# A row scan of nine-tap convolutions, with its columns kept in three phases and six sub-products of three taps in place of nine taps

## Chip, core and metric

The kernel is one program on one core of a Trainium2 chip. TensorE multiplies (PE; its weight loads are listed apart as PEld), VectorE (DVE), ScalarE (ACT) and GpSimd (POOL) work element by element, and SyncE (SP) issues most of the DMA transfers. The metric is the device time of one execution in microseconds (us), as the median of the runs shown. The profile is one other execution, recorded by the hardware profiler.

## What is computed

Four layers in a row on a float32 image batch of 4 x 128 x 128 x 128 (batch, rows, columns, channels), each as `x = x + layer(groupnorm(x))`. The first is a deformable convolution, the third a message layer, the fourth a triangle product. The change is made for the second, a scan over the 128 rows:

```
rows = jnp.moveaxis(x, 1, 0)
def step(carry, row):
    new = row + jax.nn.relu(conv1d_same(carry, W))     # 9 taps along the columns, 128 -> 128 channels
    return (new, new)
_, outs = jax.lax.scan(step, rows[0], rows[1:])
```

Each row needs the finished row before it, so the rows can't be worked side by side; the four batches can.

## The kernel before, in words

`scan_layer` (from line 966) holds channels on the 128 partitions. Per row and batch, 128 columns lie along the free dimension.

- **Loading.** `rows(y0)` (line 994) fetches four rows of layer 1's output at a time: four transfers on SP's queue, one for each batch, each 128 columns (the partitions) by four rows of 512 bytes. It is called one chunk ahead, at the first row of the chunk before.
- **Turning.** `turned` (line 1003) transposes each batch's 128 x 128 block on PE into one PSUM tile `x1T_ps`, and ACT writes the normalized row `rowT` from it, one instruction for each batch (line 1011).
- **Convolving.** The carry of one row is kept in two halves of two batches each, twice (old and new), with four zero columns at either side. For each half, nine matmuls of 256 columns (2 batches x 128) add up in one PSUM bank (line 1029). Float32 matmuls run as two passes, so the profile shows 18 of them for each half, 36 for a row.
- **Closing the row.** DVE writes the new carry half as `max(conv, 0) + rowT` (line 1040) and the layer's output `x2c` as that plus the raw row, read from `x1T_ps` (line 1045). Every fourth row DVE also takes statistics of `x2c` (line 1049), its sums over the columns (`sum_w`, line 1053) and over the rows (`part`, `sum_h`, lines 1055 and 1056), and ACT's queue issues four stores of `x2c` (line 1052).

The order within each engine is set by a scheduler from the tiles' dependences, and semaphores join the engines. While PE works on one half of a row, DVE closes the other half. PSUM has eight banks: four for `x1T_ps`, four for the convolution.

`message_and_triangle` (from line 1061) reads `x2c` back as `X`, batch by batch. Its `right` (line 1240, POOL) and its output transfers (line 1315) are the only other places that the change touches.

Of the kernel before, what the change touches and what calls it, by code (L numbers as in the profile page):

```python
# [9 lines left out]
F32 = mybir.dt.float32  # L10
# [3 lines left out]
ALU = mybir.AluOpType  # L14
AX = mybir.AxisListType
PSUM = bass.MemoryType.PSUM
DRAM = bass.MemoryType.DRAM

P = 128
B = 4  # L20
S = 128
# [9 lines left out]
TAPS = 9  # L31
NQ = 4
DQ = P // NQ
# [929 lines left out]
                nc.vector.tensor_copy(to, v)  # L963


def scan_layer(tc, c, small, x1, w, norms, x2T):

    nc = tc.nc  # L970
    RB = 4
    PAD = TAPS // 2
    WP = S + 2 * PAD
    HB = B // 2
    stats = small.tile([P, B, S // RB, 6], F32, name="stats2")
    sum_w = small.tile([P, B, S], F32, name="sum_w")
    sum_h = small.tile([P, B, S], F32, name="sum_h")
    nc.vector.memset(sum_h, 0.0)
    with ExitStack() as ctx:
        wp = ctx.enter_context(tc.tile_pool(name="l1w", bufs=1))  # L980
        two = ctx.enter_context(tc.tile_pool(name="l1two", bufs=2))
        three = ctx.enter_context(tc.tile_pool(name="l1three", bufs=3))
        ps_x = ctx.enter_context(tc.tile_pool(name="l1ps_x", bufs=4, space=PSUM))
        ps_c = ctx.enter_context(tc.tile_pool(name="l1ps_c", bufs=4, space=PSUM))

        wt = wp.tile([P, TAPS, P], F32, name="wconv")
        nc.scalar.dma_start(wt, w.rearrange("k i o -> i k o"))
        carry = [
            [wp.tile([P, HB, WP], F32, name=f"carry_{i}_{h}") for h in range(2)] for i in range(2)
        ]  # L990
        for pair in carry:
            for t in pair:
                nc.vector.memset(t, 0.0)

        def rows(y0):
            xc = three.tile([P, B, RB, S], F32, name="x1rows")
            for b in range(B):
                nc.sync.dma_start(
                    xc[:, b], x1[b, y0 : y0 + RB, :, :].rearrange("h w c -> w h c")
                )  # L1000
            return xc

        def turned(xc, i):

            px = ps_x.tile([P, B, S], F32, name="x1T_ps")
            for b in range(B):
                nc.tensor.transpose(px[:, b, :], xc[:, b, i, :], c.ident)  # L1007
            rt = three.tile([P, B, S], F32, name="rowT")
            for b in range(B):
                s, t = norms[b]  # L1010
                nc.scalar.activation(rt[:, b, :], px[:, b, :], AF.Identity, bias=t, scale=s)  # L1011
            return px, rt

        chunks = {0: rows(0)}
        ready = {0: turned(chunks[0], 0)}
        for y in range(S):
            i = y % RB
            if i == 0:
                x2c = two.tile([P, B, RB, S], F32, name="x2c")
                if y + RB < S:  # L1020
                    chunks[y + RB] = rows(y + RB)
            px, rt = ready.pop(y)
            old, new = carry[(y + 1) % 2], carry[y % 2]
            conv = []
            if y:
                for h in range(2):
                    pc = ps_c.tile([P, HB, S], F32, name="conv1_ps")
                    for k in range(TAPS):
                        nc.tensor.matmul(  # L1029
                            pc, lhsT=wt[:, k, :], rhs=old[h][:, :, k : k + S],  # L1030
                            start=(k == 0), stop=(k == TAPS - 1),
                        )
                    conv.append(pc)
            if y + 1 < S:
                ready[y + 1] = turned(chunks[(y + 1) // RB * RB], (y + 1) % RB)
            for h in range(2):
                bs = slice(h * HB, (h + 1) * HB)
                mid = new[h][:, :, PAD : PAD + S]
                if y:
                    nc.vector.scalar_tensor_tensor(  # L1040
                        mid, conv[h], 0.0, rt[:, bs, :], ALU.max, ALU.add
                    )
                else:
                    nc.vector.tensor_copy(mid, rt[:, bs, :])
                nc.vector.tensor_tensor(x2c[:, bs, i, :], px[:, bs, :], mid, ALU.add)
            if i == RB - 1:
                y0 = y + 1 - RB
                for b in range(B):
                    nc.vector.bn_stats(
                        stats[:, b, y // RB, :], x2c[:, b].rearrange("p h w -> p (h w)")  # L1050
                    )
                    nc.scalar.dma_start(x2T[b, :, y0 : y + 1, :], x2c[:, b])
                nc.vector.tensor_reduce(sum_w[:, :, y0 : y + 1], x2c, AX.X, ALU.add)
                part = two.tile([P, B, S], F32, name="part")
                nc.vector.tensor_reduce(part, x2c.rearrange("p b h w -> p b w h"), AX.X, ALU.add)
                nc.vector.tensor_tensor(sum_h, sum_h, part, ALU.add)
                chunks.pop(y0)
    return stats, sum_w, sum_h


def message_and_triangle(tc, c, x2T, counted, w2, w3, out):
# [3 lines left out]
    nc = tc.nc  # L1065
    stats2, sum_w, sum_h = counted
# [3 lines left out]
    JB = 8  # L1070
    with ExitStack() as ctx:
        wp = ctx.enter_context(tc.tile_pool(name="l3w", bufs=1))
# [30 lines left out]
        with tc.tile_pool(name="l3prep", bufs=1) as prep, tc.tile_pool(  # L1103
            name="l3ps_w", bufs=2, space=PSUM
        ) as ps_w:
            raw = prep.tile([P, NP_], F32, name="wraw")
# [3 lines left out]
            both = ((left_w, left_b), (right_w, right_b), (lgate_w, lgate_b), (rgate_w, rgate_b))  # L1110
# [30 lines left out]
        one = ctx.enter_context(tc.tile_pool(name="l3one", bufs=1))  # L1141
        two = ctx.enter_context(tc.tile_pool(name="l3two", bufs=2))
        ps_s = ctx.enter_context(tc.tile_pool(name="l3ps_s", bufs=2, space=PSUM))
        ps_a = ctx.enter_context(tc.tile_pool(name="l3ps_a", bufs=4, space=PSUM))
        ps_b = ctx.enter_context(tc.tile_pool(name="l3ps_b", bufs=2, space=PSUM))

        for b in range(B):
# [5 lines left out]
            _, _, s2, t2 = gn_part(nc, c, two, two, ps_s, stats2[:, b], "x2")  # L1153
# [47 lines left out]
            for j0 in range(0, S, 4):  # L1201
                py = ps_a.tile([P, S, 4], F32, name="cent_ps", tag="ps_a")
                nc.tensor.matmul(  # L1203
                    py, lhsT=c.center, rhs=X[:, :, j0 : j0 + 4], start=True, stop=True
# [3 lines left out]
                for j in range(4):  # L1208
                    nc.tensor.matmul(  # L1209
                        pv[:, j0 + j : j0 + j + 1], lhsT=sq[:, j, :], rhs=c.mean[:, 0:1],  # L1210
                        start=True, stop=True,
# [7 lines left out]
            for q in range(NQ):  # L1219
                left = big.tile([P, S, DQ], F32, name=f"left_{q}")  # L1220
                right = big.tile([P, S, DQ], F32, name="right")
                cols = slice(q * 4 * DQ, (q + 1) * 4 * DQ)
                for j0 in range(0, S, 4):
                    pp = ps_a.tile([P, 4, 4 * DQ], F32, name="proj_ps", tag="ps_a")
                    for j in range(4):
                        nc.tensor.matmul(  # L1226
                            pp[:, j], lhsT=X[:, :, j0 + j], rhs=wcat[:, cols], start=True, stop=True
                        )
                    pre = two.tile([P, 4, 4 * DQ], F32, name="work")
                    for j in range(4):  # L1230
                        nc.vector.scalar_tensor_tensor(  # L1231
                            pre[:, j], pp[:, j], rstd[:, j0 + j : j0 + j + 1], pbias[:, cols],
                            ALU.mult, ALU.add,
                        )
                    sig = two.tile([P, 4, 2 * DQ], F32, name="sig")
                    nc.scalar.activation(sig, pre[:, :, 2 * DQ :], AF.Sigmoid)  # L1236
                    nc.vector.tensor_tensor(
                        left[:, j0 : j0 + 4, :], pre[:, :, 0:DQ], sig[:, :, 0:DQ], ALU.mult
                    )
                    nc.gpsimd.tensor_tensor(  # L1240
                        right[:, j0 : j0 + 4, :], pre[:, :, DQ : 2 * DQ], sig[:, :, DQ:], ALU.mult
                    )
                for d0 in range(0, DQ, 4):
                    pt = ps_b.tile([P, 4, S], F32, name="tri_ps", tag="ps_b")
                    for d in range(4):
                        nc.tensor.matmul(  # L1246
                            pt[:, d], lhsT=right[:, :, d0 + d], rhs=left[:, :, d0 + d],
                            start=True, stop=True,
                        )
                    nc.scalar.copy(left[:, :, d0 : d0 + 4], pt.rearrange("p d j -> p j d"))  # L1250
                prod.append(left)
# [3 lines left out]
            for j0 in range(0, S, JB):  # L1255
# [21 lines left out]
                for h in range(0, JB, 4):  # L1277
                    pg = ps_a.tile([P, 4, P], F32, name="gate_ps", tag="ps_a")
                    for j in range(4):
                        nc.tensor.matmul(  # L1280
                            pg[:, j], lhsT=X[:, :, j0 + h + j], rhs=wcat[:, gcols],
                            start=True, stop=True,
# [16 lines left out]
                res = two.tile([P, JB, P], F32, name="res")  # L1299
                for h in range(0, JB, 4):  # L1300
# [11 lines left out]
                    nc.vector.tensor_tensor(  # L1312
                        res[:, h : h + 4], po, lastb.unsqueeze(1).to_broadcast([P, 4, P]), ALU.add
                    )
                nc.sync.dma_start(out[b, :, j0 : j0 + JB, :], res)


@with_exitstack
# [67 lines left out]
```

## Time and profile before

| what | us |
|---|---|
| median of 3 runs (8645.82 to 8707.95) | 8695.24 |
| span of the profiled execution | 8803.9 |
| of it, the scan: first load issued to the last carry written | 4489.8 to 5543.0 |
| PE busy over the span | 7117.6 (81%) |
| DVE busy over the span | 5000.0 (57%) |
| ACT busy over the span | 3346.5 (38%) |
| POOL busy over the span | 1721.0 (20%) |

The profiled execution spans 108.7 us more than the median of the timed runs; what lies around its span isn't shown apart. The profile's slices say how much of each fortieth of the span an engine was busy, and the timeline lists instructions by start and duration with, in brackets, how long the engine had been idle and what released it. A matmul's duration holds the way through the array, so matmuls in a row overlap: their pace is read from start to start.

### The profile page before, as it was taken

How to read it: one execution, taken by the hardware profiler on the slowest of the kernel's cores; microseconds unless marked ns; L12 is line 12 of the kernel's file. 1: busy time of each engine (PE TensorE's matmuls, PEld its weight loads, DVE VectorE, ACT ScalarE, POOL GpSimd, SP SyncE). 2: the span in 40 equal slices, each digit the busy share in tenths (PEclk: the TensorE clock that was granted, in tenths of full speed). 3: DMA queues.
4: the chain of work that ended last, by engine and by line, in shares of the span. 5: the costliest groups of instructions: out<-in, count | busy, mean ns of one | idle time of the engine just before them, and what ended most of it. 6: DMA issues, size and time to landing. Idle time of an engine off the chain costs nothing. (4 is left out here: it accounts for less than half of the span.)

```text
span 8803.9 us, 105220 instructions
## 1 busy us (share of the span) xinstructions
PE 7117.6 (81%) x35800; PEld 5835.4 (66%) x35800; DVE 5000.0 (57%) x13104; ACT 3346.5 (38%) x5404; POOL 1721.0 (20%) x1791
## 2 busy tenths in 40 slices
PE   0668777978789777799989999698679668966986
PEld 0556565756567556677778888398549647963985
DVE  5545555755557555577744444447626752674466
ACT  0445554555555555466621111122312312231223
POOL 0123222233222223222200000112112120212121
PEclk9778887988878888799999999688759876976897
DMA  2333333433333333343321221100100010001000
GB/s 66 88 67 77 76 74 69 98 76 80 73 72 98 72 74 76 68 80 61 64 65 60 67 67 54 53 1 10 42 25 1 20 58 1 1 29 48 1 10 29
DMA packets 978744, 473.48 MB, mean 54 GB/s; under 512 B 705076, under 2 KB 931988, under 8 KB 963860
## 3 DMA queue, kind: packets, MB, share of 16 engines
q1 hardware_dynamic: 951216, 428.93, 20.3%
q10 hardware_dynamic: 26980, 37.73, 1.2%
q8 instruction: 284, 4.65, 0.2%
q14 instruction: 264, 2.16, 0.1%
HBM read 284.15 MB, written 182.35 MB: 53 GB/s over the span
## 5 line engine op out<-in xcount | busy, mean ns | idle before, releaser
L491 PEld LDWEIGHTS v_ps<-m,pixels 120*128 120x128 f32 x11008 | 1512.9, 206 | 221.5 <-issue 69.3
L473 ACT ACTIVATE dist<-t_ps 120x780 f32<-120x780 f32 x1560 | 1266.5, 812 | 983.6 <-DVE neg L481 848.5
L491 PE MATMUL v_ps<-m,pixels 120*128 120x108 f32 (+1 forms) x11008 | 1610.0, 291 | 20.1 <-DVE v L502 14.9
L502 DVE COPY v<-v_ps 128x432 f32<-128x432 f32 x1376 | 809.6, 588 | 1390.4 <-PE v_ps L491 1386.9
L551 PE MATMUL conv_ps<-v,wneg 128*128 128x128 f32 (+2 forms) x5160 | 1382.6, 403 | 14.8 <-DVE v L507 14.8
L482 POOL TENSOR_TENSOR m<-neg,tent 120x390 f32<-120x390 f32 x688 | 700.9, 1019 | 2785.1 <-DVE neg L481 2508.1
L551 PEld LDWEIGHTS conv_ps<-v,wneg 128*128 128x128 f32 x5160 | 851.6, 205 | 305.5 <-issue 181.6
L1029 PE MATMUL conv_ps<-carry,wconv 128*128 128x256 f32 x4572 | 1009.5, 378 | 0.3 <-issue 0.3
L1029 PEld LDWEIGHTS conv_ps<-carry,wconv 128*128 128x128 f32 x4572 | 850.8, 188 | 121.3 <-issue 0.6
L475 ACT ACTIVATE tent<-dist 120x390 f32<-120x390 f32 x1560 | 823.0, 528 | 213.7 <-POOL m L482 155.9
L1226 PE MATMUL proj_ps<-wcat,X 128*128 128x128 f32 x4096 | 903.0, 384 | 0.0
L1226 PEld LDWEIGHTS proj_ps<-wcat,X 128*128 128x128 f32 x4096 | 901.5, 313 | 0.0
L1231 DVE SCALAR_TENSOR_TENSOR work<-proj_ps,rstd,pbias 128x128 f32<-128x128 f32 x2048 | 613.2, 344 | 293.3 <-issue 173.7
L464 PE MATMUL t_ps<-places,spread 14*120 14x390 bf16 x3096 | 581.4, 388 | 214.2 <-ACT dist L473 166.1
L482 DVE TENSOR_TENSOR m<-neg,tent 120x390 f32<-120x390 f32 x860 | 652.1, 758 | 91.1 <-DVE neg L481 1.4
L481 DVE TENSOR_SCALAR neg<-dist 120x390 f32<-120x390 f32 x1560 | 630.9, 414 | 42.2 <-ACT dist L473 41.2
L464 PEld LDWEIGHTS <-spread 14*120 14x120 bf16 x3120 | 221.8, 129 | 515.8 <-issue 414.8
L1011 ACT ACTIVATE rowT<-x1T_ps,t_x,s_x 128x128 f32<-128x128 f32 x512 | 192.4, 458 | 862.7 <-PE x1T_ps L1007 417.2
L371 PE MATMUL img_ps<-ident,xin 128*128 128x128 f32 x512 | 98.1, 325 | 514.4 <-DMA xin<-in_x_dram 511.5
L1240 POOL TENSOR_TENSOR right<-work,sig 128x128 f32<-128x128 f32 x512 | 240.6, 471 | 1362.4 <-ACT sig L1236 1138.0
L1303 PE MATMUL gT_ps<-ident,cen 128*128 128x128 f32 x512 | 124.0, 424 | 468.5 <-DVE cen L1298 412.1
L1236 ACT ACTIVATE sig<-work 128x256 f32<-128x256 f32 x512 | 213.4, 417 | 639.1 <-DVE work L1231 639.1
(185 smaller groups left out, 8134.4 us busy)
## 6 DMA issues: line engine op xcount, KB each, us to landing
pixels<-tab SPq DMA_DIRECT2D x688, 120.0 KB
xin<-in_x_dram SPq DMA_DIRECT2D x56, 1024.0 KB
tab<-rows SPq DMA_DIRECT2D x384, 128.0 KB
x<-x1c SPq DMA_DIRECT2D x32, 1024.0 KB
x1rows<-x SPq DMA_DIRECT2D x128, 256.0 KB
x2T<-x2c ACTq DMA_DIRECT2D x128, 256.0 KB
X<-x2T SPq DMA_DIRECT2D x16, 2048.0 KB
out_dram<-res SPq DMA_DIRECT2D x64, 512.0 KB
```

The costliest lines, as they stand in the source:

```text
L464: nc.tensor.matmul(tp[0:LANES, d, 0:n].rearrange("p (r c) -> p r c", c=PADW), lhsT=spread[p0 : p0 + 14, :], rhs=src[p0 : p0 + 14, k, :, 0: ...
L473: nc.scalar.activation(dist[:, :, 0:n], tp[0:LANES, :, 0:n], AF.Abs)
L475: nc.scalar.activation(tent[:, 0:n], dist[:, 0, 0:n], AF.Relu, bias=1.0, scale=-1.0)
L481: nc.vector.tensor_scalar(neg[:, 0:n], dist[:, 1, 0:n], 1.0, 1.0, ALU.min, ALU.subtract)
L482: engine.tensor_tensor(m, neg[:, 0:n], tent[:, 0:n], ALU.mult)
L491: nc.tensor.matmul(vp[:, h * n : h * n + rows * w].rearrange("p (k c) -> p k c", c=w), lhsT=pix[0:LANES, xb, :], rhs=m[:, :, RX * xb : RX ...
L502: nc.vector.tensor_copy(v[:, :, c0 : c0 + full * RX].rearrange("p k (h c) -> p k h c", c=RX), vp[:, 0 : full * n].rearrange("p (h k c) -> ...
L551: nc.tensor.matmul(pc[:, at : at + r1 - r0, :], lhsT=wneg[:, 3 * ky + kx, :], rhs=v[:, k0 + kx, r0:r1, kx : kx + S], start=m == 0, stop=m ...
L1029: nc.tensor.matmul(pc, lhsT=wt[:, k, :], rhs=old[h][:, :, k : k + S], start=(k == 0), stop=(k == TAPS - 1),)
L1226: nc.tensor.matmul(pp[:, j], lhsT=X[:, :, j0 + j], rhs=wcat[:, cols], start=True, stop=True)
L1231: nc.vector.scalar_tensor_tensor(pre[:, j], pp[:, j], rstd[:, j0 + j : j0 + j + 1], pbias[:, cols], ALU.mult, ALU.add,)
L1240: nc.gpsimd.tensor_tensor(right[:, j0 : j0 + 4, :], pre[:, :, DQ : 2 * DQ], sig[:, :, DQ:], ALU.mult)
```

## The change

The columns are kept by their number modulo three: phase 0 has 43 of them, phase 1 43 and phase 2 42. Written so, a nine-tap convolution is a three-by-three arrangement of three-tap convolutions of phases, and a known identity forms the three output phases from six three-tap products in place of nine, some of them on sums of phases and with sums of weights. Each product takes all four batches at once: 172 columns (176 for the one named `edge`), three matmuls, two passes each.

- The carry becomes one tile for all batches with six slots: the three phases (0, 1, 2) and three sums (3 = 0+1, 4 = 1+2, 5 = 0+1+2).
- DVE closes a row with twelve instructions of 172 elements in place of four of 256, and ACT copies one product (`m1`) out of PSUM first.
- The output `x2c` and the sums over rows move to POOL: three additions of 172 elements and one of 512 a row. ACT makes a copy `raw` of the turned row for it, as POOL is given no PSUM tile.
- `rows` loads each batch in three transfers, one for each phase, of 43, 43 and 42 partitions. Two chunks are loaded before the first row, and each later chunk is called for at the first row of the chunk before it, as until now. The stores of `x2c` go from ACT's queue to SP's.
- An order written by hand (`manual_schedule`) makes each engine run the scan's instructions in the order of the program text.
- Later, `right` and the output are put back into natural column order: `right` in two POOL instructions where a group of columns crosses a phase, and the output in transfers of 512-byte pieces.

```diff
+        less2 = wp.tile([P, PHASES, P], F32, name="less2")
+        nc.vector.tensor_scalar(less2, taps[:, 2], -1.0, None, ALU.mult)
...
             for b in range(B):
-                nc.sync.dma_start(
-                    xc[:, b], x1[b, y0 : y0 + RB, :, :].rearrange("h w c -> w h c")
-                )
+                for p in range(PHASES):
+                    nc.sync.dma_start(
+                        xc[FIRST[p] : FIRST[p] + COUNT[p], b],
+                        x1[b, y0 : y0 + RB, p:S:PHASES, :].rearrange("h w c -> w h c"),
+                    )
...
+            raw = three.tile([P, B, S], F32, name="rawT")
+            nc.scalar.copy(raw, px)
+            return rt, raw
...
+        def product(to, terms):
+            n = to.shape[2]
+            todo = [(wgt[:, a], src, at + a) for wgt, src, at in terms for a in range(PHASES)]
+            for i, (wgt, src, at) in enumerate(todo):
+                nc.tensor.matmul(
+                    to, lhsT=wgt, rhs=src[:, :, at : at + n],
+                    start=i == 0, stop=i + 1 == len(todo),
+                )
...
+        ctx.enter_context(tc.manual_schedule(engines=order))
+        chunks = {0: rows(0), RB: rows(RB)}
...
             if y:
-                for h in range(2):
-                    pc = ps_c.tile([P, HB, S], F32, name="conv1_ps")
-                    for k in range(TAPS):
-                        nc.tensor.matmul(
-                            pc, lhsT=wt[:, k, :], rhs=old[h][:, :, k : k + S],
-                            start=(k == 0), stop=(k == TAPS - 1),
-                        )
-                    conv.append(pc)
+                pa = ps_a.tile([P, B, N + 1], F32, name="edge_ps")
+                product(pa, [(less2, old[:, 0], 1), (taps[:, 0], old[:, 2], 0)])
+                ps = {}
+                for name, wgt, at in (
+                    ("m1", taps[:, 1], 1), ("m01", both["w12"], 3), ("m12", both["w01"], 4),
+                    ("m012", both["w012"], 5),
+                ):
+                    ps[name] = ps_m.tile([P, B, N], F32, name=f"{name}_ps")
+                    product(ps[name], [(wgt, old[:, at], 1)])
             if y + 1 < S:
-                ready[y + 1] = turned(chunks[(y + 1) // RB * RB], (y + 1) % RB)
...
+                ready[y + 1] = turned(y + 1)
+            if y:
+                m1 = two.tile([P, B, N], F32, name="m1")
+                nc.scalar.copy(m1, ps["m1"])
+                e = two.tile([P, B, N], F32, name="e")
+                nc.vector.tensor_tensor(e, ps["m01"], m1, less)
+                y0 = two.tile([P, B, N], F32, name="y0")
+                nc.vector.tensor_tensor(y0, pa[:, :, 0:N], e, add)
+                nc.vector.scalar_tensor_tensor(
+                    kept(new, 0), y0, 0.0, part(rt, 0), ALU.max, add
+                )
+                f = two.tile([P, B, N], F32, name="f")
+                nc.vector.tensor_tensor(f, ps["m12"], m1, less)
...
+                nc.vector.tensor_tensor(y2[:, :, 0:n2], f[:, :, 0:n2], pa[:, :, 1 : 1 + n2], less)
+                nc.vector.scalar_tensor_tensor(
+                    kept(new, 2), y2[:, :, 0:n2], 0.0, part(rt, 2), ALU.max, add
+                )
+                nc.vector.tensor_tensor(e, e, f, add)
...
+                nc.vector.tensor_tensor(y1, ps["m012"], e, less)
+                nc.vector.scalar_tensor_tensor(
+                    kept(new, 1), y1, 0.0, part(rt, 1), ALU.max, add
+                )
...
+            if y + 1 < S:
+                nc.vector.tensor_tensor(kept(new, 3, N), kept(new, 0, N), kept(new, 1, N), add)
+                nc.vector.tensor_tensor(kept(new, 4, N), kept(new, 1, N), kept(new, 2, N), add)
+                nc.vector.tensor_tensor(kept(new, 5, N), kept(new, 3, N), kept(new, 2, N), add)
+            for p in range(PHASES):
+                nc.gpsimd.tensor_tensor(
+                    part(x2c[:, :, i], p), part(raw, p), kept(new, p), add
+                )
+            nc.gpsimd.tensor_tensor(sum_h, sum_h, x2c[:, :, i], add)
             if i == RB - 1:
...
-                    nc.scalar.dma_start(x2T[b, :, y0 : y + 1, :], x2c[:, b])
-                nc.vector.tensor_reduce(sum_w[:, :, y0 : y + 1], x2c, AX.X, ALU.add)
-                part = two.tile([P, B, S], F32, name="part")
-                nc.vector.tensor_reduce(part, x2c.rearrange("p b h w -> p b w h"), AX.X, ALU.add)
-                nc.vector.tensor_tensor(sum_h, sum_h, part, ALU.add)
-                chunks.pop(y0)
+                    nc.sync.dma_start(x2T[b, :, r0 : y + 1, :], x2c[:, b])
+                nc.vector.tensor_reduce(sum_w[:, :, r0 : y + 1], x2c, AX.X, ALU.add)
+                chunks.pop(r0)
...
-                    nc.gpsimd.tensor_tensor(
-                        right[:, j0 : j0 + 4, :], pre[:, :, DQ : 2 * DQ], sig[:, :, DQ:], ALU.mult
-                    )
+                    at = 0
+                    for n, ws_ in columns(j0, 4):
+                        nc.gpsimd.tensor_tensor(
+                            right[:, ws_, :], pre[:, at : at + n, DQ : 2 * DQ],
+                            sig[:, at : at + n, DQ:], ALU.mult,
+                        )
+                        at += n
...
-                nc.sync.dma_start(out[b, :, j0 : j0 + JB, :], res)
+                at = 0
+                for n, ws_ in columns(j0, JB):
+                    nc.sync.dma_start(out[b, :, ws_, :], res[:, at : at + n])
+                    at += n
```

## Prediction, made before the changed kernel ran

> **What bounds it now.** I read the busy shares by slice first (they place the scan between 4489 and 5551 us), then the scan's stretches:
>
> ```profile
> core 0: us, PE busy (x) PEld busy (x) DVE busy (x) ACT busy (x) POOL busy (x), PEclk, DMA share, GB/s
> 4489.00:5551.00 1062.00, 1047.14 (x5084) 912.73 (x5084) 497.54 (x741) 192.39 (x512) 0.00 (x0) 0.99 0.20 65
> 6202.63:6212.87 10.24, 7.88 (x43) 7.69 (x42) 7.63 (x23) 3.76 (x4) 0.00 (x0) 1.00 0.13 53
> 6212.87:6219.70 6.83, 1.96 (x9) 1.71 (x9) 4.18 (x6) 1.81 (x3) 2.34 (x1) 0.50 0.00 1
> ```
>
> PE is busy for 99% of the scan at a granted clock of 0.99; POOL does nothing there, and DVE and ACT have room. The other two stretches, from the last layer, come back below for the clock. Then the timeline of one row:
>
> ```profile
> 5007.87 0.60 PE L1007 MATMUL x1T_ps<-ident,x1rows 128*128 128x128 f32 x4
> ...
> 5008.31 7.94 PE L1029 MATMUL conv_ps<-carry,wconv 128*128 128x256 f32 x36
> 5008.50 2.01 SPq L998 DMA_DIRECT2D x1rows<-x  x4
> 5008.53 0.42 DVE L1045 TENSOR_TENSOR x2c<-x1T_ps,carry 128x256 f32<-128x256 f32 x1
> 5008.56 1.50 ACT L1011 ACTIVATE rowT<-x1T_ps,t_x,s_x 128x128 f32<-128x128 f32 x4 [6.70 <-issue]
> 5012.47 0.42 DVE L1040 SCALAR_TENSOR_TENSOR carry<-conv_ps,rowT 128x256 f32<-128x256 f32 x1 [3.51 <-PE conv_ps L1029]
> ```
>
> 36 matmuls in 7.94 us, the last of 0.38, are 216 ns from start to start; four transposes pace at 109. A row is 36 x 0.216 + 4 x 0.109 = 8.22 us. DVE closes the first half (5012.47) while PE works on the second: the recurrence costs PE nothing. Prices for what comes:
>
> ```profile
> 6200.45 0.59 ACT L1305 COPY gT<-gT_ps 128x512 f32<-128x512 f32 x1 [4.82 <-PE gT_ps L1303]
> 5575.69 1.26 POOL L1178 TENSOR_TENSOR X<-X,work 128x512 f32<-128x512 f32 x1 [1142.81 <-DVE work L1175]
> L1240 POOL TENSOR_TENSOR right<-work,sig 128x128 f32<-128x128 f32 x512 | 240.6, 471 | 1362.4 <-ACT sig L1236 1138.0
> L1056 DVE TENSOR_TENSOR sum_h<-sum_h,part 128x512 f32<-128x512 f32 x31 | 21.1, 682 | 0.0
> L1045 DVE TENSOR_TENSOR x2c<-x1T_ps,carry 128x256 f32<-128x256 f32 x256 | 108.6, 424 | 14.8 <-ACT rowT L1011 0.4
> ```
>
> **PE's part.** In the trace, matmuls of 128, 256 and 384 columns start 112, 216 and 322 ns apart at full clock, 0.81 ns a column. So 172 columns are 148 ns and 176 are 151: 24 x 0.148 + 12 x 0.151 + 0.44 for the transposes = 5.80 us a row, 2.42 less than now. If all else lay beside it, the scan would lose 127 x 2.42 = 307 us.
>
> **What stands behind the m1 copy.** It doesn't lie beside it. In the text, and so on each engine, `turned(y+1)` comes before the copy of `m1`. On PE the transposes of row y+1 stand behind all 36 matmuls of row y; on ACT four `rowT` and `raw` wait for those transposes, and the `m1` copy waits behind them. The first DVE instruction, `e`, needs that copy. So DVE begins on a row when PE has finished all of it, and PE's next product needs phase 0 of DVE's result. Going round one row:
> - PE: 5.80, plus 0.16 for the last pass to come out (0.38 - 0.22) and about 0.3 of waits inside (the second half of `edge` and `m1` need phases 2 and 1, each three DVE instructions after the phase before, against 0.9 us of matmuls): 6.25.
> - ACT: 0.09 to start, four `rowT` 1.50, `raw` 0.59 less 0.11 of overlap (four of 0.457 take 1.50), `m1` about 0.34 (0.59 less 340 elements at 0.73 ns, the slope between 390 and 780 elements, 0.528 and 0.812 us) less 0.11: 2.30.
> - DVE: 256 and 512 elements are 0.424 and 0.682, so 172 are 0.34. A dependent one starts 0.04 after the end of the one before (8.49 to 8.53 above). `e`, `y0` and phase 0: 1.10; 0.15 for two handovers.
>
> Together 9.8 us against 8.22, at full clock. In that circle PE idles about 3.7 us a row. The clock in this trace changes only at steps of 3.41 us, between 1 and 0.5; of the 145 times it fell, nine in ten followed a step with PE under 49% busy. 3.7 us of idling always leaves one such step, and then PE restarts cold for one to two steps: 1.5 to 3 us of work lost in a row, 2.0 in the mean. I take 11.8 us a row, with 9.8 and 12.8 as ends.
>
> The Trainium skill ("TensorE: Matmul & The Clock Gate", section "HAM oscillation — how this bites in real kernels") has only gaps beyond about 3.4 us re-throttle PE. By it, few of these rows would be cold and a row would stay near 9.8; I hold to the row of the trace, where partly idle steps were enough.
>
> **The loads, one engine each.** The trace holds, for every transfer, the updates of its semaphore: one from each DMA engine that took part, and one for the rest. Transfers whose outer dimension is 128 or 32 have 16, 30 or 15 have 16 (15 + 1), 12 or 72 have 13 (12 + 1), 4 have 5. All fit the largest divisor up to 16. The twelve-piece transfers of outer dimension 4 (`off<-parts`), issued one after another, never have more than four pieces under way: the same four engines each time. 43 is prime; by that pattern its transfers run on one engine, the same one, and only the 42-partition ones on 14.
>
> The same is stated by the Trainium skill ("DMA: Bandwidth & Descriptors", section "Why a DMA increments its semaphore by 16 and not by 1"), down to one engine for 127 partitions; no transfer here has a prime count.
>
> A 512-byte piece keeps an engine busy for 28 ns (mean of the scan's loads; the pace of all 16 was 24 at its densest, 35 over whole chunks: 128 pieces on each in 4.5 us). A chunk brings 8 transfers of 172 pieces to the one engine, 1376 x 0.028 = 38.5 us, and 4 x 12 x 0.028 = 1.3 from the others; now it is 128 pieces, 3.6. Nearest rows as ends: four engines, 9.6 us; 24 and 35 ns, 33 and 48.
>
> Nor is there time for it. The loads stand on SP behind the four stores of the chunk before, which wait for POOL at the end of its last row; they are needed by the transposes four rows later, which also hold up (through ACT) the last of those rows. Round a chunk, from POOL's end to the next:
> - issue to the first piece 1.0 (5008.50 to 5009.52); the stores' share, 4 x 8 pieces of 85 ns, 2.7; the loads 39.8; landing 0.8: 44.3
> - the last transposes and handover 0.4; ACT 2.2; nine DVE instructions to phase 1 (9 x 0.34 and six handovers of 0.04, less two overlaps) 3.2; POOL's two last additions, 0.56 each between 0.471 and 1.26, 1.2: 7.0
>
> 51.3 us, against 4 x 11.8 = 47 by the rows: the loads end last. Over the scan: the first two chunks land 42 and 82 us after the first issue (the second is needed by the end of row 3), plus 7: 89. Then 30 x 51.3 = 1539 and a last chunk without loads, 47: 1675 us, against 1054 now (4489.8 to 5543.5). **+621.**
>
> **Small parts.** On DVE, statistics and `sum_w` (4 x 0.69 + 2.27) every fourth row lie in the 6 us in which DVE waits for PE; without that cover they would be 1.2 a row. DVE and POOL delay each other where both read two SBUF tiles: DVE's line 482 takes 0.57 alone and 1.21 beside POOL's. Here the three sums of phases (slots 3 to 5) meet POOL's additions; PE needs the last of them 1.8 us after it is due, so I take 0, at most 0.6 a row if all three meet one, inside the 4.3 us that rows have to spare per chunk. ACT's queue loses the stores; SP gains them, and their wait for POOL has the loads behind it, as counted. The weight sums (four DVE instructions, under 1 us each) hide under the first load. After the scan 4.4 us of DVE's sums go and 1.3 of POOL come: -3. In the last layer 32 more POOL pieces of about 0.4 us lie in its 1362 us of idling before `right`; output pieces fall from 4096 to 512 bytes, 1024 x 28 / 16 = 1.8 us of each engine for 8 columns that take 18 us of work: 0. All together **+618**: 8804 becomes 9422 in the profile, and 8695 becomes 9313 (the profile spans 109 more than the median; I add the same to both).
>
> **Rivals.**
> - *The loads spread over several engines* (by 4-engine rows, 9.6 us): then the circle through ACT decides. 127 x (11.8 - 8.22) = +455, 9150; at a full clock 127 x 1.6 = +203, 8900. For it: no prime count in the trace. Against: the divisors fit every transfer.
> - *One engine alone is slower than one among 16.* At 35 ns: 51.3 + 1424 x 0.007 = 61.3, 30 x 10 more, 9615. For it: `off<-parts` pieces take 164 ns at best but often 600 beside three others.
> - *Faster: PE goes on while DVE closes the row.* The place is ACT's queue: were `m1` copied before `rowT` of the next row, and the loads spread, PE would be the bound at 5.80 to 6.4 us: 8390 to 8460. It decides as soon as the circle is under 8.22, which needs 1.6 us out of 9.8 at full clock. The order is in the text; only a wrong reading of it gives this.
> - *About the same*: loads spread, and ACT and DVE prices a third too high: 8.2 to 8.9.
>
> **How the numbers follow.** Loads on one engine at 24 to 32 ns, 9140 to 9480: 0.60, the forecast. Slower engine: 0.13. Loads spread: 0.19, of it 0.07 below 8970. Faster 0.03, the same 0.05 (within 1%, 87 us, about what three runs that scatter over 62 us can tell). The range 8970 to 9580 leaves out the 0.07 and 0.08 on the low side and some 0.05 above. Slower by over 1%: 0.92.
>
> **What would show it.** Right: matmuls of 172 columns 146 to 150 ns apart at full clock; the `m1` copy always directly behind `raw`, and `e` waiting on it; one row in four with PE or ACT waiting 5 to 15 us on `x1rows`; two semaphore updates for a 43-partition load; 51 us from the stores of one chunk to the next; a granted clock near 0.7. Wrong: 16 updates or loads that land in 5 us; `e` beside PE's products; a scan under 1250 us; a row of the same length whether or not it opens a chunk.

## The result, and the profile after

| what | before | after |
|---|---|---|
| median, us (4 runs each) | 8699.74 (8645.82 to 8707.95) | 9253.08 (9214.93 to 9260.66) |
| span of the profiled execution | 8803.9 | 9245.3 |
| the scan: first load issued to last carry written | 1053.3 | 1615.5 |
| four rows, from stores to stores (median) | 32.89 | 49.56 |

The ratio is 1.0623, 95% interval 1.0575 to 1.0671: 553 us slower. The scan alone is 562 longer. The busy times of the scan without its first load, of the kernel after (the columns are those of the same view before):

```profile
core 0: us, PE busy (x) PEld busy (x) DVE busy (x) ACT busy (x) POOL busy (x), PEclk, DMA share, GB/s
4512.00:6083.00 1571.00, 1053.33 (x5076) 1019.81 (x5076) 698.36 (x1678) 277.38 (x763) 389.47 (x509) 0.77 0.13 42
```

The identity did what it says: two thirds of the columns go through PE in about as many matmuls. Yet PE is busy for as many microseconds as before, in a window half as long again, because the granted clock fell from 0.99 to 0.77. No engine is the bound any more; the row is a chain. One row of the kernel after, cut from the timeline:

```profile
5002.08 2.85 PE L1057 MATMUL m_ps<-carry,w 128*128 128x172 f32 x18
5004.77 0.60 PE L1038 MATMUL x1T_ps<-ident,x1rows 128*128 128x128 f32 x4
5005.40 1.50 ACT L1042 ACTIVATE rowT<-x1T_ps,t_x,s_x 128x128 f32<-128x128 f32 x4 [9.91 <-PE x1T_ps L1038]
5006.79 0.59 ACT L1044 COPY rawT<-x1T_ps 128x512 f32<-128x512 f32 x1
5007.25 0.33 ACT L1089 COPY m<-m_ps 128x172 f32<-128x172 f32 x1
5007.61 0.34 DVE L1091 TENSOR_TENSOR e<-m_ps,m 128x172 f32<-128x172 f32 x1 [2.68 <-ACT m L1089]
...
5008.85 2.10 PE L1057 MATMUL edge_ps<-carry,less 128*128 128x176 f32 x6 [3.48 <-DVE carry L1094]
...
5011.03 0.69 DVE L1116 TENSOR_TENSOR carry<-carry 128x172 f32<-128x172 f32 x1
...
5012.35 1.05 PE L1057 MATMUL m_ps<-carry,wconv 128*128 128x172 f32 x6
...
5018.77 0.34 DVE L1091 TENSOR_TENSOR e<-m_ps,m 128x172 f32<-128x172 f32 x1 [6.45 <-ACT m L1089]
```

Read it downwards. PE finishes the last products of the row and the transposes of the next; ACT then does `rowT` four times, `raw`, and only after these the copy `m1` (the view leaves numbers out of names, so it shows `m`); DVE starts 0.03 us after that copy; PE stands idle for 3.48 us until the new phase 0 is written, and then makes six passes of 176 columns in 2.10 us, half clock; six of 172 at full clock take 1.05, at 5012.35. From one `e` to the next are 11.16 us, and 12.36 and 14.10 in the two rows that follow. All of this repeats, as the waits of the same window say (what was waited for, then us in total, times, and the longest):

```profile
ACT rowT L1042 <- PE x1T_ps L1038: 1261.8, 124, 13.6
...
DVE e L1091 <- ACT m L1089: 820.4, 126, 11.0
...
PE edge_ps L1057 <- DVE carry L1094: 443.4, 126, 3.9
...
PE x1T_ps L1038 <- DMA x1rows<-x: 74.1, 31, 4.0
```

PE waits for DVE's new phase 0, and so for ACT's copy ahead of it, in 126 of 127 rows, 3.5 us each. On the loads it waits in 31 rows, once for each chunk, 2.4 us. The loads of 43 partitions send two updates of their semaphore, one of them when all of the data has landed, against 16 for a load before; the 42-partition ones send 15. The 2048 pieces of 512 bytes of a chunk take 37.5 us from the first to the last.

### The profile page after: what moved, and what is told of

Read it like the earlier page. It is cut to its first block, busy times and chain, and to the rows that moved or that the text cites. A ratio compares the mean times of both kernels' runs of the same rounds, so it can differ in the third digit from the quotient of the medians.

```text
span 9245.3 us, 107809 instructions
## 1 busy us (share of the span) xinstructions
PE 7011.0 (76%) x35800; PEld 5867.4 (63%) x35800; DVE 5209.1 (56%) x14057; ACT 3431.7 (37%) x5659; POOL 2115.7 (23%) x2335
## 5 line engine op out<-in xcount | busy, mean ns | idle before, releaser
L1057 PE MATMUL edge_ps<-carry,less 128*128 128x176 f32 x762 | 258.1, 510 | 444.5 <-DVE carry L1094 443.4
L1316 POOL TENSOR_TENSOR right<-work,sig 128x128 f32<-128x128 f32 (+3 forms) x544 | 246.4, 456 | 1254.2 <-ACT sig L1310 1029.8
L1119 POOL TENSOR_TENSOR x2c<-rawT,carry 128x172 f32<-128x172 f32 (+1 forms) x384 | 229.9, 612 | 1275.6 <-DVE carry L1094 979.1
L1091 DVE TENSOR_TENSOR e<-m_ps,m 128x172 f32<-128x172 f32 x127 | 42.8, 337 | 823.7 <-ACT m L1089 820.4
L1057 PEld LDWEIGHTS edge_ps<-carry,less 128*128 128x128 f32 x762 | 204.1, 315 | 470.3 <-issue 466.7
```

The lines of the kernel that those rows point to most:

```text
L1057: nc.tensor.matmul(to, lhsT=wgt, rhs=src[:, :, at : at + n], start=i == 0, stop=i + 1 == len(todo),)
L1316: nc.gpsimd.tensor_tensor(right[:, ws_, :], pre[:, at : at + n, DQ : 2 * DQ], sig[:, at : at + n, DQ:], ALU.mult,)
```

## The experiments

The theory was the prediction's: the `m1` copy, behind ACT's work for the next row, closes a circle through PE, ACT and DVE in which PE idles and loses its clock; loads on one DMA engine add to it. Rivals were that one of the two is everything, or that the clock is.

| kernel | scan, us | four rows, us | scan at half clock | time, us (runs) |
|---|---|---|---|---|
| before | 1053.3 | 32.89 | 1% | 8699.74 (4) |
| after | 1615.5 | 49.56 | 47% | 9253.08 (4) |
| loads cut | 1504.2 | 47.15 | 43% | 9197.86 (1) |
| `m1` first | 1290.2 | 39.51 | 41% | 8941.89 (1) |
| both | 891.2 | 27.70 | 12% | 8543.05 (4) |
| loads cut, PE kept busy | 1268.7 | 39.41 | 1% | 8893.76 (1) |
| before, its loads cut at 43 and 86 | 1332.5 | 40.18 | 19% | 8931.22 (1) |
| both, statistics spread | 770.7 | 23.65 | 3% | 8397.21 (4) |
| the same, `var_ps` 128 columns wide | 771.3 | 23.63 | 3% | 8315.06 (4) |

**The loads cut** so that each part's partitions divide well: 32 + 11, or 32 + 10.

```diff
+                    for at, n in ((0, 32), (32, COUNT[p] - 32)):
+                        w0 = p + PHASES * at
...
```

> The changed kernel with each load of 43 or 42 partitions cut into one of 32 and one of 11 or 10, so that 16 and 11 (10) DMA engines take them; nothing else differs. In the changed kernel's profile the scan takes 1614 us from its first load to its last carry, four rows 49.5, of which PE waits about 2.4 on the loads. Theory (the circle PE - ACT - DVE of a row is nearly as long as the loads on one engine): the waits on the loads go, the first chunks land in under 20 us in place of 80, four rows take 47 us and the scan 1490 to 1530; 27 updates of semaphores are replaced by 17 and 12 to a pair of transfers. Rival (the loads alone made the scan long): four rows fall towards 33 us and the scan under 1200.

Measured: scan 1504.2, four rows 47.15, and from 4530 to 5300 us not one wait of PE on the loads. The loads cost 111 us of the 562: 2.41 in each of 30 chunks, 72, as the circle is nearly as long as they are, and the remaining 39 where the first two chunks are waited for. The rows alone make the kernel slow: without the waits on the loads its scan is still 451 us longer than before.

**`m1` first:** the copy before ACT's work for the next row, the loads as they were.

```diff
+                m1 = two.tile([P, B, N], F32, name="m1")
+                nc.scalar.copy(m1, ps["m1"])
             if y + 1 < S:
                 ready[y + 1] = turned(y + 1)
             if y:
-                m1 = two.tile([P, B, N], F32, name="m1")
-                nc.scalar.copy(m1, ps["m1"])
```

> The changed kernel with ACT's copy of m1 ahead of the next row's rowT and raw, so that DVE can begin on a row while PE still works on it; the loads stay as they are, most on one DMA engine. Theory (both the place of the copy and the one engine hold the scan): the circle falls to about 6.4 us a row, and the one engine's 37.5 us of loads and 2.7 of stores a chunk are what is left: four rows take 40 to 42 us, PE waits 10 us or more for x1rows in each chunk, the scan takes 1290 to 1360 us. Rival (the copy's place doesn't matter, DVE's twelve instructions and POOL do): four rows stay at 47 to 50.

Measured: scan 1290.2, four rows 39.51. Its waits, from 4530 to 5300 us:

```profile
DVE e L1091 <- PE m_ps L1057: 307.0, 78, 13.7
...
PE x1T_ps L1038 <- DMA x1rows<-x: 266.7, 39, 8.9
```

DVE no longer waits for ACT's copy but for the product itself, and PE waits for the loads, 13.7 us in each of the 19.5 chunks of the window. 39.51 is the 37.5 us that one engine needs for a chunk, and 2 us. With the circle gone, the loads are the bound.

**Both edits.**

> Both edits at once: loads spread and the copy of m1 early. Theory: neither limit is left; a row costs what PE needs, 5.8 us, or DVE and POOL in the rows that close a chunk: 6.0 to 6.8 us a row, the scan 780 to 880 us against 1054 before the change, the whole kernel 170 to 270 us faster than before the change, 8430 to 8530. The granted clock in the scan is back over 0.95. Rival (the clock stays low or DVE and POOL hold each other up): 7.5 us a row or more, and no gain on the kernel before.

Measured: 8543.05 us, ratio 0.9792 (0.9723 to 0.9862) to before, so the change in this form is some 1.4 to 2.8% faster than the kernel before. Scan (891.2) and time lie just above the ranges expected, and the clock in the scan, 0.94, just below; the timeline shows why:

```profile
4900.29 2.26 DVE L1134 TENSOR_REDUCE sum_w<-x2c 128x16 f32<-128x2048 f32 x1
...
4902.47 0.32 DVE L1095 TENSOR_TENSOR e<-m_ps,m 128x172 f32<-128x172 f32 x1
...
4903.68 2.02 PE L1061 MATMUL edge_ps<-carry,less 128*128 128x176 f32 x6 [2.62 <-DVE carry L1098]
...
4909.29 0.34 DVE L1095 TENSOR_TENSOR e<-m_ps,m 128x172 f32<-128x172 f32 x1 [2.12 <-PE m_ps L1061]
```

In one row out of four DVE does the statistics of the chunk in one block, four of 0.69 and the 2.26 here, and `e` comes only then; PE idles 2.62 us, and goes on at half clock. That row takes 10.2 us, the three others 5.83 each. The prediction had this block in DVE's idle 6 us and named its price without that cover, 1.2 us a row; (27.70 − 23.65) / 4 = 1.0 is what the last step below gives back.

**PE kept busy:** the loads cut, and before each row's first product eleven matmuls (22 passes) on constants, whose result is overwritten. The circle stays; only the idling goes.

```diff
+                flat = wt.rearrange("i k o -> i (k o)")[:, 0 : B * (N + 1)]
+                for k in range(11):
+                    nc.tensor.matmul(
+                        pa, lhsT=wt[:, k % TAPS, :],
+                        rhs=flat.rearrange("i (b n) -> i b n", b=B),
+                        start=True, stop=True,
+                    )
```

> The run with spread loads (four rows 47.2 us, 43% of the scan at half clock), plus eleven matmuls on constant operands (22 passes of 176 columns, 3.3 us at full clock) ahead of each row's first product, in the 3.5 us in which PE waits for DVE; they write the PSUM tile that the product then overwrites. Theory (the idle part of a row drops the clock, and PE restarts cold): the clock stays at 1, the share of the scan at half clock falls under 0.1, a row costs the 9.8 to 10.2 us of the prediction at full clock, four rows 39 to 41 and the scan 1250 to 1320 us, though PE has 22 passes more to do. Rival (the clock isn't what makes a row 11.8 us): four rows stay at 47 or grow.

```profile
4904.15 3.45 PE L1083 MATMUL edge_ps<-wconv 128*128 128x176 f32 x22
...
4906.20 0.34 ACT L1100 COPY m<-m_ps 128x172 f32<-128x172 f32 x1
...
4907.78 1.17 PE L1061 MATMUL edge_ps<-carry,less 128*128 128x176 f32 x6 [0.18 <-DVE carry L1105]
```

The filler ends 0.18 us before phase 0 is there, so it delays nothing, and the six passes take 1.17 us in place of 2.10. Scan 1268.7, four rows 39.41. More work on PE made the scan 235 us shorter than with the loads cut alone: the half clock costs (47.15 − 39.41) / 4 = 1.94 us a row, and the circle at full clock is 39.41 / 4 = 9.85.

**Before, its loads cut** into 43, 43 and 42 neighbouring columns, and nothing else: the loads' part by itself.

```diff
+                for w0, w1 in ((0, 43), (43, 86), (86, S)):
+                    nc.sync.dma_start(
+                        xc[w0:w1, b], x1[b, y0 : y0 + RB, w0:w1, :].rearrange("h w c -> w h c")
+                    )
```

> The kernel before the change, its loads of four rows cut into 43, 43 and 42 neighbouring columns; all else as before. Theory (a transfer of 43 partitions runs on one DMA engine, at 27 to 28 ns for 512 bytes): the one engine has 37.5 us of loads and 2.7 of stores for each chunk, against 32.9 us in which PE needs it: four rows take 40 to 42 us, the scan 1320 to 1380 us against 1054, and PE waits 7 to 9 us a chunk for x1rows. Rival (such transfers spread like others): the scan stays within 40 us of 1054.

The waits from 4530 to 5300 us:

```profile
ACT rowT L1012 <- DMA x1rows<-x: 461.6, 32, 77.6
...
PE conv_ps L1030 <- DVE carry L1041: 114.2, 19, 37.8
```

Scan 1332.5, four rows 40.18: 279 us of loss from 43 partitions alone, in a kernel whose arithmetic is untouched. The first line is ACT's idle time, most of which costs nothing; the second is where the late loads reach PE, once a chunk, through `rowT` and the carry. From 4700 to 5700 us PE idles 4.4 us a chunk, less than the 7 to 9 expected; the rest of the 7.3 us that a chunk grew by came while PE was at work, with 19% of the scan at half clock. The same bytes on 16 engines hid entirely (32.89 for four rows).

**The statistics spread:** both edits, and DVE takes the statistics of the chunk before, one batch after each row.

```diff
+        def counted(t, r0, b):
+            nc.vector.bn_stats(
+                stats[:, b, r0 // RB, :], t[:, b].rearrange("p h w -> p (h w)")
+            )
+            nc.vector.tensor_reduce(sum_w[:, b, r0 : r0 + RB], t[:, b], AX.X, ALU.add)
...
+            if due:
+                counted(due[0], due[1], i)
```

> Spread loads and early m1, and the statistics of a chunk (four of 0.69 us and the sum over columns of 2.27 us) no longer in one block after its last row but one batch after each row of the next chunk. In the run with both edits a chunk takes 27.7 us: three rows of 5.83 and one of about 10.2, where DVE comes to e late by its block and PE restarts cold. Theory: DVE's 1.0 us of idling in a row takes most of the 1.3 us that now comes to each row: rows of 5.9 to 6.4, a chunk 23.6 to 25.6, the scan 770 to 840 us against 891, the kernel 8410 to 8500. Rival (DVE is the bound, its busy time the same): no more than 20 us gained.

```profile
4905.11 2.84 PE L1061 MATMUL m_ps<-carry,w 128*128 128x172 f32 x18
...
4905.50 0.68 DVE L1069 BATCH_NORM_STATS2 stats<-x2c 128x6 f32<-128x512 f32 x1
4906.10 0.66 DVE L1072 TENSOR_REDUCE sum_w<-x2c 128x4 f32<-128x512 f32 x1
4906.69 0.32 DVE L1102 TENSOR_TENSOR e<-m_ps,m 128x172 f32<-128x172 f32 x1
...
4908.23 1.07 PE L1061 MATMUL edge_ps<-carry,less 128*128 128x176 f32 x6
```

The two pieces lie while PE still works on the products, and PE goes on without a gap. A row is 23.65 / 4 = 5.91 us, against PE's own 5.80; the kernel 8397.21, ratio 0.9661 (0.9609 to 0.9713).

**The centring loop, four runs.** The profile before spanned 109 us more than the median, and that led to another place. In the last layer, PE repeats for each batch a loop of `cent_ps` and `var_ps` (lines 1277 and 1283 after), which nothing of the change touches. In the kernel after, these windows hold all but the last rounds of the four loops:

```profile
6223.00:6279.00 56.00, 55.97 (x303) 39.84 (x304) 1.34 (x7) 18.67 (x32) 0.00 (x0) 0.96 0.00 1
6983.00:7088.00 105.00, 104.89 (x303) 72.54 (x304) 0.00 (x0) 18.56 (x32) 0.00 (x0) 0.50 0.00 0
7792.00:7897.00 105.00, 105.00 (x304) 72.41 (x305) 0.00 (x0) 18.51 (x31) 0.00 (x0) 0.50 0.00 0
8600.00:8655.00 55.00, 55.00 (x303) 39.24 (x304) 0.00 (x0) 18.51 (x31) 0.00 (x0) 0.97 0.00 1
```

303 of a loop's 320 passes take 55 or 56 us, or 105, PE always busy, at full clock but for the first microseconds or at half clock throughout. From its first pass to the end of its last a loop takes 59 to 60 us or 111; these whole times are given below, while the expectations count as the windows do. In the profile before, all four took 111. All runs on this start from the version with the statistics spread. The first put 14 matmuls of 512 columns ahead of each loop, to have the clock up when it begins.

```diff
+            for k in range(14):
+                keep_ps = ps_a.tile([P, 512], F32, name="keep_ps", tag="ps_a")
+                nc.tensor.matmul(
+                    keep_ps, lhsT=mwide, rhs=wcat[:, 0:512], start=True, stop=True
+                )
```

> As the run with spread statistics, plus, in the last layer, fourteen matmuls on constant operands for each batch ahead of the centring loop, into a PSUM tile that nobody reads, while PE waits 15 us for ACT. In every run so far each of the four centring loops took either 55 or 105 us, by whether it began and stayed at half clock. Theory: warmed up, all four take 55 to 57 us; the kernel's median falls by 50 to 150 us against the run without, and its runs scatter less than 25 us. Rival (the loop itself is too thin to hold the clock): loops of 105 us remain.

It failed: the loops took 111, 60, 60 and 111 us, and the kernel 8415.79 us (ratio 0.9693, 0.9653 to 0.9734), 19 more than without. The filler ended some 5 us before the loop, whose first matmul still waited for ACT, and all four loops began at half clock:

```profile
5390.07 0.28 PE L132 MATMUL gn_ps<-gp_mv,gmean 128*128 128x1 f32 x2
5391.18 0.38 PE L140 MATMUL gn_ps<-gp_d,gmean 128*128 128x1 f32 x2 [0.83 <-DVE gp_d L138]
5395.31 3.78 PE L1294 MATMUL cent_ps<-X,center 128*128 128x512 f32 x4 [3.75 <-ACT X L1272]
```

The next theory looked at what the passes do: two of 512 columns, then eight of one column each. At full clock a pass of one column paces at 110 ns and one of 128 at 112, but the first streams almost nothing.

```diff
-            pv = ps_b.tile([P, S], F32, name="var_ps", tag="ps_b")
+            pv = ps_b.tile([P, 2 * S], F32, name="var_ps", tag="ps_b")
...
-                        pv[:, j0 + j : j0 + j + 1], lhsT=sq[:, j, :], rhs=c.mean[:, 0:1],
+                        pv[:, j0 + j : j0 + j + 128], lhsT=sq[:, j, :], rhs=c.mean[:, 0:128],
```

> The kernel with loads cut, m1 first and the statistics spread, and in the last layer's centring loop each matmul of var_ps writes 128 equal columns instead of one (the next one overwrites all but its first, so the result is the same; at full clock 128 columns pace at 0.112 us, one column at 0.110, so the loop costs the same). The loop repeats two passes of 512 columns (0.83 us at full clock) and eight of one column (0.88 us): PE is always at work, but columns stream for 48% of the time. Theory: the clock counts streamed columns, and a loop at 48% stands on the edge (nine in ten falls of the clock followed a step under 49% busy), so it may stay at half clock for all of its 105 us. Then 128 columns take it off the edge: all four loops 55 to 62 us, the kernel about 2 x 49 us below the 8397 of the one without, 8280 to 8350. Rival: how PE enters the loop (after 13 to 15 us of idling) sets its state, whatever it streams: some loops still 105 us, 8350 to 8420.

> The same with 32 columns in each matmul of var_ps: columns stream for (0.83 + 8 x 32 x 0.00081 us) / 1.75 = 59% of the loop. If streamed columns are counted with an edge near 49%, all four loops 55 to 62 us as with 128 columns, 8280 to 8350; if the entry decides, some loops stay at 105 us.

With 128 columns all four loops took 60 to 62 us, and the kernel 8317.48 (ratio 0.9570, 0.9537 to 0.9604). With 32 columns they took 59, 110, 110 and 59, and the kernel 8416.95 (0.9672, 0.9636 to 0.9707): the expected edge near 49% fell, since 59% wasn't enough. And with 128 columns the scheduler had also changed the order on PE, to rounds of four and sixteen passes. So the two were taken apart, with PE's order in this loop written by hand: one column in the new order (the first loop below), and 128 columns in the old (the second).

```diff
+            with tc.manual_schedule(engines={mybir.EngineType.PE}):
+                for j0 in range(0, S, 8):
+                    sqs = [centred(j0), centred(j0 + 4)]
+                    summed(j0, sqs[0])
+                    summed(j0 + 4, sqs[1])
...
+                for j0 in range(0, S, 4):
+                    if j0 + 4 < S:
+                        sqs[j0 + 4] = centred(j0 + 4)
+                    summed(j0, sqs.pop(j0))
```

> One column in each matmul of var_ps, as in the kernel with the statistics spread, but in the order that the wide ones had got: two matmuls of cent_ps (four passes), then eight of var_ps (sixteen passes), written by hand for PE. Theory that the columns streamed decide: 48% of the time as before, so some of the four centring loops still take 105 us. Rival, the order decides (a round of four and sixteen passes doesn't fall in step with the clock's 3.41 us, as a round of two and eight does, which takes 3.42 at half clock): all four loops 55 to 62 us.

> 128 columns in each matmul of var_ps, in the old order: one matmul of cent_ps (two passes), four of var_ps (eight passes). Theory that the columns streamed decide: PE streams all the time, and all four loops take 55 to 62 us. Rival, the order decides: some loops still take 105 us.

The windows of the loops, first with one column in the new order, then with 128 in the old:

```profile
5393.00:5499.00 106.00, 106.00 (x309) 73.08 (x310) 1.77 (x8) 18.19 (x32) 0.00 (x0) 0.50 0.00 1
6204.00:6297.00 93.00, 92.82 (x303) 63.06 (x303) 0.00 (x0) 18.12 (x31) 0.00 (x0) 0.57 0.00 0
```

```profile
5387.00:5444.00 57.00, 56.99 (x314) 40.77 (x315) 1.34 (x7) 19.25 (x33) 0.00 (x0) 0.97 0.00 1
6146.00:6203.00 57.00, 57.00 (x306) 40.55 (x307) 0.00 (x0) 18.51 (x31) 0.00 (x0) 0.95 0.00 1
```

One column: 112, 99, 111 and 62 us (8457.53 in one run). 128 columns: 58 to 59 in all four (8315.06, ratio 0.9555, 0.9493 to 0.9617). The columns decide, not the order. Nor is it the pace: at half clock a pass starts 0.21 us after the one before with one column as with 128, so that a round takes 3.41 us with either. With the 8317.48 above, which differs by less than the runs scatter, this is the best version of the whole, 387 us below the median of the kernel before in the same set of runs (8701.58).

## Why the prediction was right

It said slower, by 618 us, and the kernel is slower by 553. Point by point:

- **PE's part** held. The transposes start 2.69 us after the eighteen passes of 172 columns before them began (5002.08 to 5004.77): 149 ns each, where 148 were worked out from the widths of the trace before.
- **The circle** held to its size. 9.8 us at full clock were predicted and 9.85 measured with PE kept busy. The loads cut alone left a scan 451 us longer than before; the prediction's rival "loads spread" had 455.
- **The clock**: 2.0 us a row were predicted, 1.94 measured. Its rule, that partly idle steps of 3.41 us are enough, held against the Trainium skill ("TensorE: Matmul & The Clock Gate", "HAM oscillation — how this bites in real kernels"), which names gaps beyond about 3.4 us. The gaps after the change, 3.5 us in the mean, don't tell the two apart; the 31 gaps of 2.60 to 2.89 us in the kernel with both edits do, as PE came out of 24 of them at half clock. One figure of the rule was misread: by PE's busy time 114 of the 145 falls before the change followed a step under 49%, and nine in ten one under 63%; 49% is the figure for the weight loads. It cost nothing, as after the change all 126 falls in the scan followed a step at most 35% busy. The granted clock was 0.77, and "near 0.7" too low.
- **The loads**: one engine, as the divisors of the trace said, and as the skill's "DMA: Bandwidth & Descriptors" has it ("Why a DMA increments its semaphore by 16 and not by 1"); the two updates for 43 partitions confirm both. Here the size was off: the term of 51.3 us a chunk measured 49.56, mainly as the pieces took 37.5 and not 39.8 us (27 ns for one in the median, and starts 23 ns apart). Over 30 chunks that is 52 of the 59 us by which the scan was overestimated (+621 against +562). PE's wait on the loads was 2.4 us a chunk. The sign "5 to 15" didn't follow from the prediction's own sum, which leaves 51.3 - 47.2 = 4.1; with the measured 49.56 and 47.15 the 2.4 come out. Loads and rows came closer to a tie than the sum had them.
- **The small parts**: DVE beside POOL was put at nothing, at most 0.6 us a row. The contention is there (0.69 us at 5011.03 for what takes 0.34 alone, in two instructions a row), and hides, as assumed: with it a row still takes 5.91 us in the version with the statistics spread.
- **The profile's own offset**: 109 us were added to both sides as if they belonged to the kernel. The profile before has all four centring loops at half clock, which costs 51 us each; the profile after has two. So the forecast for the profile, 9422, was 177 too high: 59 of that is the scan and some 102 the two loops. The median's forecast doesn't rest on the offset, as it was the median before plus 618. That a median run before has two such loops fewer than the profile would fit the 109, but the timed runs before left no trace to show it.

Where the 562 us of the scan come from, in the order in which the runs took them away: 111 from loads on one engine (1615.5 to 1504.2), 235 from the half clock (to 1268.7), 215 from the circle at full clock (to the 1053.3 before); the prediction had 166, 254 and 203 (rounded, of 621). In another order the parts differ: loads and rows cover each other, and the loads by themselves cost the kernel before 279.

The rival "faster" needed both `m1` first and the loads spread, and gave 8390 to 8460. With both, 8543 was measured: it had left out DVE's block of statistics, which the prediction elsewhere hid in DVE's waiting. With that spread too, 8397. The 307 us that fewer passes could bring were there (scan 1053.3 to 770.7, 283 us), behind three things that the change had put on the path.

## What to carry to other kernels

Fewer passes on a bound engine pay only while the rest of the recurrence hides behind it: write down the circle from an engine's last result to its next input, with every instruction queued ahead of each link, and put the one instruction that the circle needs ahead of the ones that only the next row needs. Choose tile cuts whose partition counts divide well (32 + 11, not 43): a transfer that was hidden can become the bound without a byte more. And when PE must wait, look at the granted clock of its next passes: here filling the wait with work that is thrown away left the wait as long and still gave back 1.94 us a row.

## What the runs showed of the hardware

A loop that keeps PE busy without a gap can stay at half clock for all of its 111 us, or rise at its start and take 59 to 60, with the same program. With eight of ten passes one column wide, 24 of the 40 loops in ten profiled executions were at half clock, nearly all of them from end to end; with 128 columns, which cost no time at full clock (a round of two and eight passes takes 1.75 us either way), none of the eight loops in two executions was. 32 columns weren't enough. Where between 32 and 128 the edge lies wasn't tried.

The state of a narrow loop goes with its place in the clock's steps. The clock changes only at steps of 3.41 us, which lie on one even grid from the first to the last in each of the thirteen profiles, and all the loops begin at half clock. Of the 40 narrow loops, the 23 whose first pass came 1.37 to 2.80 us before the next step stayed at half clock to the end; the 17 with 0.17 to 1.01 us, or 3.05 to 3.17, rose at that step or at the one after (one of them, in the new order, fell back 14 us later). With 128 columns, five loops began 1.97 to 2.21 us before a step, and all five rose. With 32 columns one at 1.37 rose, too, and those at 1.87 and 2.22 stayed. No edit set the place, and why it matters wasn't tested. A loop opens with four passes of 512 columns, 3.6 us at half clock, and each round after them takes 3.41 us at half clock, just one step, so no later step differs from the one before. (In the new order a round at half clock takes 6.83 us, two steps, so it falls in step as well, against what the rival in its expectation assumed.)

Steps of 51 us would also account for part of the scatter between runs of one kernel, 8645.82 against 8695.24 before, though the timed runs before left no trace to show it. Another part lies ahead of the scan, which begins between 4458 and 4490 us in the thirteen profiles, with nothing before it changed.
